# The x side of a gated recurrence: two four-step matmul groups become one eight-step block of seven half-width products

## The chip, the cores and the metric

One core of one Trainium2 chip runs the kernel. The metric is the device time of one execution in microseconds (us). The kernel before took 1693.7 us (median of three runs, 1693.68 to 1693.88). Differences within about 0.2% (3.4 us) are treated as no change.

## The reference

A gated recurrence runs over 512 steps for a batch of 8, with 512 inputs and a state h of 512 values, all float32. Its output is added to the input.

```
def step(h, x_t):
    fused = sigmoid(concat([x_t, h]) @ w_W + w_b)            # 1024 x 1024
    r, z = split(fused, 2)
    memory = x_t @ wx_W + wx_b + r * (h @ wh_W + wh_b)
    h_new = z * h + (1 - z) * tanh(memory)
return x + all h_new
```

Each step so needs an x side (x_t times the upper half of `w_W` and `wx_W`: 512 x 1536, which depends on nothing but the input) and an h side (h times the lower half of `w_W` and `wh_W`: 512 x 1536, which depends on the step before).

## The kernel before, in words

**Layout.** The 512 units are split into four quarters k of 128 (the contraction, on partitions) and each output of 512 into four parts j of 128. A matmul has 32 columns of data as its stationary operand and weights as its moving one, and writes partitions 32j to 32j+31 of PSUM. So four matmuls with j = 0 to 3 use four different column groups of TensorE, and every loop over j (`for j in range(NQ)`) issues four of them in a row. All matmuls go through the helper `mm`, line 178. Float32 matmuls leave two records each, a weight load and a matmul twice.

**h side, once a step.** `ORDER` is "R0 R1 G0 G1 R2 R3 G2 G3 H0 H1 H2 H3": three PSUM banks (R: the reset gate; G and H: the update gate and h @ wh) times four k, four matmuls of 128 columns each, 48 a step. Quarters 0 and 1 of the state lie in tile hTA, 2 and 3 in hTB.

**x side.** The x of four steps times 8 rows makes the 32 stationary columns of a *group* g. `prefill(g)` issues 16 matmuls of 384 columns (k = 0 to 3, j = 0 to 3) into columns 64 to 447 of the PSUM bank `xps[g % 2]`, which ScalarE has filled with the bias before (`seed`, line 213, a copy of 128x512). The x side is written out as a generator, `later`, and is worked off in program order behind the h side: after H3 of each step `take(later, 1)` issues the four matmuls of one k; step 0 takes four such. ScalarE later copies columns of `xps` into the R, G and H banks of the group (`spread`, line 230, 128x128 each, one a step for three steps), and VectorE transposes its X columns into `md1` (`turn_x`, line 235). The matmuls of the h side then add to what lies in R, G and H.

**The recurrence.** In each step, VectorE and ScalarE turn PSUM into the next state, in a fixed order: transposes of R (`tr`, line 303), sigmoid on ScalarE (line 205) into md0A and md0B, transposes of G (`md1A`, line 321, and `tz`), a scan that makes memory for half A (line 283), tanh, and a scan that makes the new hTA. Half B follows in the same way with H. R0 of the next step waits for hTA, R2 and R3 for the two parts of hTB. At the end of a step ScalarE does two copies of the new state and then the `spread` or `seed` of that step; VectorE does `turn_x` and three tiny memsets (line 383); GpSimd adds x to the new state for the output (line 385, two additions of 128x16). `turn_r` of half B waits for GpSimd's additions of eight steps before.

The order on every engine is written by hand (`manual_schedule`).

Of the kernel before, what the change touches and what calls it, by code (L numbers as in the profile page):

```python
# [7 lines left out]
F32 = mybir.dt.float32  # L8
BF16 = mybir.dt.bfloat16
AF = mybir.ActivationFunctionType  # L10
ALU = mybir.AluOpType
PSUM = bass.MemoryType.PSUM

P = 128
NQ = 4
GS = 4
B = 8
# [11 lines left out]
FIRST = "Q0 x Q1 x Q2 x Q3 H0 H1 H2 H3"  # L29

BANKS = ("R", "G", "H")

XP = {"G": slice(0, 128), "R": slice(128, 256), "X": slice(256, 384), "H": slice(384, 512)}

# [2 lines left out]
def tile_cond_rnn_residual(  # L37
# [39 lines left out]
    nc = tc.nc  # L77
    NCH = x.shape[0]
    T = NCH * TC
    NG = T // GS  # L80

    const = ctx.enter_context(tc.tile_pool(name="const", bufs=1))
# [13 lines left out]
    def load_x(c, half=slice(0, 2)):  # L96

        if c < NCH:
            if c not in xins:
                xins[c] = xin_p.tile([P, 2, NQ, TC * B // 2], F32, tag="xin", name=f"xin_{c}")  # L100
            nc.sync.dma_start(
                out=xins[c][:, half], in_=x[c].rearrange("p (e k n) -> p e k n", e=2, k=NQ)[:, half]
            )

    def x_of(c, k, t, n):

        e, t = divmod(t, TC // 2)
        if c == 0 and e == 0:
            first = head[:, :NX].rearrange("p (k n) -> p k n", k=NQ)
            return first[:, k, t * B : (t + n) * B]  # L110
        return xins[c][:, e, k, t * B : (t + n) * B]
# [6 lines left out]
    wx = const.tile([P, NQ, NQ, 384], F32, name="wx")  # L118
# [10 lines left out]
    def wh(bank, k, j):  # L129
        return whh[:, k, j] if bank == "H" else wgr[:, k, j, {"G": slice(0, 128), "R": slice(128, 256), "Q": slice(0, 256)}[bank]]  # L130
# [3 lines left out]
    def pair(n, name, rows, slots):  # L134

        if n == "A":
            return const.tile([P, rows, 2, slots], F32, name=name)
        return const.tile([P, 2, rows, slots], F32, name=name).rearrange("p c n s -> p n c s")
# [7 lines left out]
    md1 = [[pair(n, f"md1{n}{i}", 32, 2) for i in range(2)] for n in "AB"]  # L146
# [15 lines left out]
        nc.gpsimd.memset(t_[:, :, :, 1], -1.0)  # L162
    idle = const.tile([P, IDLE], F32, name="idle")

    def state(hf, i, slot=2):

        s = i % GS
        return hT[hf][i % NH][:, B * s : B * s + B, :, slot]

    ctx.enter_context(tc.manual_schedule())  # L170
    banks = [
        {n: psum.tile([P, 128], F32, name=f"{n}{q}") for n in BANKS}
        for q in range(2)
    ]
    xps = [psum.tile([P, 512], F32, name=f"xp{q}") for q in range(2)]

    def mm(out_, lhsT, rhs, start=False):
        nc.tensor.matmul(  # L178
            out_, lhsT, rhs, start=start, stop=False, skip_group_check=True
        )  # L180
# [4 lines left out]
    def warm():  # L185

        mm(xps[1], zeros[:, :128], zeros)
# [4 lines left out]
    bias = const.tile([P, 512], F32, name="bias")  # L192
    nc.vector.tensor_copy(bias, xps[0])
    for hf in range(2):
        for slot in (0, 2):
            nc.vector.tensor_copy(
                state(hf, 0, slot), hin[:, 2 * hf : 2 * hf + 2].rearrange("p c b -> p b c")
            )
# [12 lines left out]
    def seed(g):  # L211

        nc.scalar.copy(xps[g % 2], bias)

    def prefill(g):

        c, t0 = divmod(g * GS, TC)
        for k in range(NQ):
            for j in range(NQ):
                mm(  # L220
                    xps[g % 2][32 * j : 32 * j + 32, 64:448],
                    x_of(c, k, t0, GS),
                    wx[:, k, j, :],
                )
            yield

    def spread(g, names):

        for n in names:
            nc.scalar.copy(banks[g % 2][n], xps[g % 2][:, XP[n]])  # L230

    def turn_x(g, e):

        c0 = XP["X"].start + 32 * e
        nc.vector.transpose(
            md1[e // 2][g % 2][:, :, e % 2, 1], xps[g % 2][:, c0 : c0 + 32]
        )

    def take(it, n=None):
        while n is None or n > 0:  # L240
            if next(it, it) is it:
                return
            n = None if n is None else n - 1

    def x_side():
        for g in range(1, NG):
            yield from prefill(g)

    seed(1)
    take(prefill(0))  # L250
    warm()
    later = x_side()
    spread(0, "RGH")
    for e in range(NQ):
        turn_x(0, e)

    pool_done = {}
    for i in range(T):
        g, s = divmod(i, GS)
# [6 lines left out]

        for n in (ORDER if i else FIRST).split():
            if n == "x":
                take(later, 1)
                continue  # L270
            bank, k = n[0], int(n[1])
            hs = hT[k // 2][i % NH][:, :, k % 2, 2]
            for j in range(NQ):
                to = xps[0][:, :256] if bank == "Q" else ps[bank]
                mm(to[32 * j : 32 * j + 32, :], hs, wh(bank, k, j))
        take(later, 1)

        rows = slice(B * s, B * s + B)

# [57 lines left out]
        def memory(hf):  # L337

            m = work.tile([P, B, 2, 2] if hf == 0 else [P, 2, B, 2], F32, tag=f"m{hf}", name=f"m{hf}_{i}")
            if hf == 1:  # L340
                m = m.rearrange("p c n s -> p n c s")
            for c_ in scans(hf, m, md0[hf][g % 2][:, rows], md1[hf][g % 2][:, rows]):
                act(("n", hf, c_.start, i % NH), state(hf, i, 1)[:, :, c_], m[:, :, c_, 1], AF.Tanh)
# [16 lines left out]
        if i == T - 1:  # L360
            nc.gpsimd.tensor_tensor(
                ot[:, t, :2, :].rearrange("p c n -> p n c"),
                x_of(c, slice(0, 2), t, 1).rearrange("p c n -> p n c"),
                state(0, T),
                ALU.add,
            )
# [6 lines left out]
        if i < 3:  # L373
            load_x(i + 1)

        if g + 1 < NG:
            turn_x(g + 1, s)
            if s < 3:
                spread(g + 1, "RGH"[s])
            elif g + 3 < NG:  # L380
                seed(g + 3)
        for n in range(IDLE):
            nc.vector.memset(idle[:, n : n + 1], 0.0)
        def add(hf, engine):
# [97 lines left out]
```

## Time and profile before

| what | value |
|---|---|
| median of the runs | 1693.7 us |
| profiled execution: span from its first to its last instruction | 1691.7 us |
| outside the span, against the median of the runs | 2.0 us |
| TensorE matmul records busy | 1680.3 us, 99% of the span |
| VectorE busy | 1087.0 us, 64% |
| ScalarE busy | 915.5 us, 54% |
| GpSimd busy | 231.2 us, 14% |
| granted TensorE clock | 1.000 |

PE is TensorE's matmuls, PEld its weight loads, DVE is VectorE, ACT is ScalarE, POOL is GpSimd. A row of the timeline is the start in us, the length in us, then engine, source line, operation, output and inputs, shape and the number of records that were merged into it; in brackets stands how long the engine was idle before, and what ended that. The length of a row of matmuls holds the pipeline's depth too, so rows overlap; the distance between two starts is what counts.

### The profile page before, as it was taken

How to read it: one execution, taken by the hardware profiler on the slowest of the kernel's cores; microseconds unless marked ns; L12 is line 12 of the kernel's file. 1: busy time of each engine (PE TensorE's matmuls, PEld its weight loads, DVE VectorE, ACT ScalarE, POOL GpSimd, SP SyncE). 2: the span in 40 equal slices, each digit the busy share in tenths (PEclk: the TensorE clock that was granted, in tenths of full speed). 3: DMA queues.
4: the chain of work that ended last, by engine and by line, in shares of the span. 5: the costliest groups of instructions: out<-in, count | busy, mean ns of one | idle time of the engine just before them, and what ended most of it. 6: DMA issues, size and time to landing. Idle time of an engine off the chain costs nothing.

```text
span 1691.7 us, 121258 instructions
## 1 busy us (share of the span) xinstructions
PE 1680.3 (99%) x53230; PEld 1467.6 (87%) x53230; DVE 1087.0 (64%) x8229; ACT 915.5 (54%) x5121; POOL 231.2 (14%) x1032
## 2 busy tenths in 40 slices
PE   8999999999999999999999999999999999999998
PEld 6888888888888888888888888888888888888887
DVE  5666666666666666666666666666666666666666
ACT  3555555555555555555555555555555555555554
POOL 0111111111111111111111111111111111111111
PEclk9999999999999999999999999999999999999999
DMA  4000000000000000000000000000000000000000
GB/s 177 17 17 5 17 17 17 17 4 17 17 17 17 4 17 17 17 17 13 9 18 17 17 17 4 17 17 17 17 5 17 17 17 17 4 17 11 11 11 10
DMA packets 11483, 30.86 MB, mean 18 GB/s; under 512 B 1220, under 2 KB 1732, under 8 KB 10952
## 3 DMA queue, kind: packets, MB, share of 16 engines
q1 hardware_dynamic: 10800, 22.94, 3.9%
q8 instruction: 416, 6.82, 1.7%
q14 instruction: 115, 0.94, 0.2%
q10 hardware_dynamic: 152, 0.16, 0.0%
HBM read 14.70 MB, written 8.39 MB: 14 GB/s over the span
## 4 chain that ended last, share of the span: by engine, by line
PE 98%; DMA 1%; DVE 0%; ACT 0%; issue 0%; SPq 0%
PE R L178 26%; PE G L178 26%; PE H L178 26%; PE xp L178 19%; DMA whh<-in_whh_dram 1%; DMA head<-in_xh_dram 0%; DVE md1A L321 0%; DVE hTA L283 0%; ACT hd0A L205 0%; ACT hTA L205 0%; SPq L124 0%; DVE tz L303 0%; ACT hTB L205 0%; DVE hTB L283 0%; ACT hd0B L205 0%
## 5 line engine op out<-in xcount | busy, mean ns | idle before, releaser
L178 PE MATMUL xp<-wx,xin 128*32 128x384 f32 x4032 | 431.3, 486 | 0.0
L178 PEld LDWEIGHTS R<-wgr,hTA 128*32 128x32 f32 x8176 | 247.4, 135 | 206.8 <-DVE hTA L283 206.4
L303 DVE STREAM_TRANSPOSE tr<-R 128x64 f32<-128x64 f32 x1022 | 194.4, 229 | 309.1 <-PE R L178 309.1
L178 PE MATMUL R<-wgr,hTA 128*32 128x128 f32 x8176 | 330.9, 273 | 2.2 <-DVE hTA L283 2.2
L178 PE MATMUL H<-whh,hTA 128*32 128x128 f32 x8192 | 331.3, 273 | 0.8 <-DMA whh<-in_whh_dram 0.8
L178 PE MATMUL H<-whh,hTB 128*32 128x128 f32 x8192 | 331.2, 273 | 0.0
L178 PE MATMUL R<-wgr,hTB 128*32 128x128 f32 x8176 | 330.6, 273 | 0.0
L178 PE MATMUL G<-wgr,hTB 128*32 128x128 f32 x8176 | 330.6, 273 | 0.0
L178 PE MATMUL G<-wgr,hTA 128*32 128x128 f32 x8176 | 330.6, 273 | 0.0
L385 POOL TENSOR_TENSOR ot<-xin,hTB 128x16 f32<-128x16 f32 x503 | 126.4, 251 | 1415.6 <-DVE hTB L283 1324.0
L205 ACT ACTIVATE hd0B<-tz 128x16 f32<-128x16 f32 x512 | 114.9, 224 | 305.3 <-DVE tz L303 305.3
L205 ACT ACTIVATE md0A<-tr 128x16 f32<-128x16 f32 x512 | 119.6, 234 | 265.2 <-DVE tr L303 265.2
L178 PEld LDWEIGHTS H<-whh,hTA 128*32 128x32 f32 x8192 | 260.2, 136 | 1.2 <-DMA whh<-in_whh_dram 1.2
L178 PEld LDWEIGHTS G<-wgr,hTA 128*32 128x32 f32 x8176 | 259.8, 136 | 0.0
L178 PEld LDWEIGHTS H<-whh,hTB 128*32 128x32 f32 x8192 | 254.5, 122 | 0.0
L178 PEld LDWEIGHTS G<-wgr,hTB 128*32 128x32 f32 x8176 | 254.1, 122 | 0.0
L178 PEld LDWEIGHTS R<-wgr,hTB 128*32 128x32 f32 x8176 | 245.2, 122 | 0.0
L283 DVE TENSOR_TENSOR_SCAN hTA<-hd0A,hTA 128x48 f32<-128x48 f32 x512 | 132.1, 258 | 149.2 <-ACT hTA L205 149.2
L283 DVE TENSOR_TENSOR_SCAN hTB<-hd0B,hTB 128x24 f32<-128x24 f32 x1024 | 158.1, 196 | 104.0 <-ACT hTB L205 104.0
L205 ACT ACTIVATE hd0A<-tz 128x16 f32<-128x16 f32 x512 | 118.9, 232 | 111.4 <-DVE tz L303 111.4
L321 DVE STREAM_TRANSPOSE md1A<-G 128x64 f32<-128x64 f32 x511 | 156.8, 307 | 28.7
L205 ACT ACTIVATE hTB<-hTB 128x16 f32<-128x16 f32 x512 | 121.2, 237 | 81.1 <-DVE hTB L283 80.5
(62 smaller groups left out, 1680.2 us busy)
## 6 DMA issues: line engine op xcount, KB each, us to landing
xin<-in_x_dram SPq DMA_DIRECT2D x31, 256.0 KB, 3.8
out_dram<-ot SPq DMA_DIRECT2D x31, 256.0 KB, 3.3
wx<-in_wx_dram SPq DMA_DIRECT2D x4, 768.0 KB, 7.2
wgr<-in_wgr_dram SPq DMA_DIRECT2D x4, 512.0 KB, 9.7
whh<-in_whh_dram SPq DMA_DIRECT2D x1, 768.0 KB
whh<-in_wh_dram SPq DMA_DIRECT2D x1, 256.0 KB, 11.2
out_dram<-ot SPq DMA_DIRECT2D x1, 192.0 KB, 1.9
head<-in_xh_dram ACTq DMA_DIRECT2D x1, 144.0 KB, 5.2
```

Source lines behind the costliest of these rows:

```text
L178: nc.tensor.matmul(out_, lhsT, rhs, start=start, stop=False, skip_group_check=True)
L205: inst = nc.scalar.activation(out_, in_, func, **kw).ins
L283: nc.vector.tensor_tensor_scan(*[t_[:, :, c_].rearrange("p n c s -> p (n c s)") for t_ in (out_, d0, d1)], 0.0, ALU.mult, ALU.add,)
L303: inst = nc.vector.transpose(t_.rearrange("p c n -> p (c n)"), raw[n][hf]).ins
L321: nc.vector.transpose(md1[hf][g % 2][:, :, :, 0].rearrange("p n c -> p c n"), raw["h"][hf])
L385: return engine.tensor_tensor(ot[:, t, 2 * hf : 2 * hf + 2, :].rearrange("p c n -> p n c"), x_of(c, slice(2 * hf, 2 * hf + 2), t, 1).rearr ...
```

## The change

The change works on blocks of eight steps (two groups) instead of four. Write x of the block as four blocks x_nk (n: first or second four steps; k: first or second half of the 512 inputs) and the weights as four blocks w_kc (k as before; c: columns 64 to 255 or 256 to 447, 192 each). The four results x_n0 w_0c + x_n1 w_1c take eight products in the old way. The new way takes seven products of sums of blocks, and adds results to one another:

- GpSimd makes four sums of weights once, in steps 0 to 3 (`weight_sum`, 128x1536 each), and four sums of x for each block (`x_sum`, 128x64 each, in the last four steps of the block two before).
- `products(o)` issues seven products of 2 k times 4 j matmuls of 192 columns, 56 for a block. They go to four regions, AL and BE in `xps[0]`, GA and DE in `xps[1]`.
- What the products share is carried by ScalarE's copies from region to region (AL from the bias, DE from a difference of biases, BE from AL, GA from BE, each 128x192) and by GpSimd's additions of the SBUF tile `both` (a copy of DE) to `even` and `odd`, which hold the second 192 columns of a group in SBUF.
- `turn_x` and the `spread` of H read `even` and `odd` instead of PSUM.
- Groups 0 to 3 keep the old `prefill`. Steps 0 to 4 take two of its k each where before they took one (step 0 has three more before that, as before), and from step 5 on each step takes seven of the 56 matmuls, so that j goes on from where the last step left it: 0 1 2 3 0 1 2, then 3 0 1 2 3 0 1, and so on.

```
+def products(o):
+    t_ = [q[o % 2] for q in sx]
+    for to, lhs, rhs in (
+        (AL, x_half(o, 0, 0), wx_of(0, 0)),
+        (DE, t_[0], tw[0]),
+        (BE, t_[1], tw[1]),
+        (AL, x_half(o, 0, 1), wx_of(1, 0)),
+        (GA, t_[2], tw[2]),
+        (BE, t_[3], wx_of(1, 1)),
+        (GA, x_half(o, 1, 1), tw[3]),
+    ):
+        for k in range(2):
+            for j in range(NQ):
+                mm(reg(to)[32 * j : 32 * j + 32], lhs[:, k], rhs[:, k, j])
+                yield
...
 def x_side():
-    for g in range(1, NG):
-        yield from prefill(g)
+    for o in range(2, NG // 2):
+        yield from products(o)
...
-        take(later, 1)
+        if i < 5:
+            take(first[(i + 3) // 2], 2)
+        else:
+            take(later, 7)
...
+        o, u = divmod(i, 2 * GS)
+        nxt, two = o + 1 < NG // 2, o + 2 < NG // 2
+        if i == 0:
+            nc.scalar.copy(odd[0], xps[1][:, 256:512])
         if g + 1 < NG:
             turn_x(g + 1, s)
-            if s < 3:
-                spread(g + 1, "RGH"[s])
-            elif g + 3 < NG:
-                seed(g + 3)
+        if i == 0:
+            spread(1, "R")
+        if u == 0:
+            spread(2 * o + 1, "G")
+            if o and nxt:
+                nc.scalar.copy(reg(GA), reg(BE))
+        elif u == 1:
+            spread(2 * o + 1, "H")
+        elif u == 2 and o == 0:
+            seed(3)
+            nc.scalar.copy(even, xps[0][:, 256:512])
+        elif u == 2 and nxt:
+            last = odd[(o + 1) % 2][:, :HALF]
+            nc.scalar.copy(last, reg(GA))
+            nc.gpsimd.tensor_tensor(last, last, both, ALU.add)
+        elif u == 3 and nxt:
+            if o:
+                nc.scalar.copy(even[:, :HALF], reg(BE))
+                nc.gpsimd.tensor_tensor(even[:, :HALF], even[:, :HALF], both, ALU.add)
+            spread(2 * o + 2, "R")
+        elif u == 4 and nxt:
+            if o == 0:
+                nc.scalar.copy(odd[1], xps[1][:, 256:512])
+            spread(2 * o + 2, "G")
+            if two:
+                nc.scalar.copy(reg(AL), bias[:, AL[1]])
+                x_sum(o + 2, 0)
+        elif u == 5 and nxt:
+            spread(2 * o + 2, "H")
+            if two:
+                nc.scalar.copy(reg(DE), step_bias)
+                x_sum(o + 2, 1)
+        elif u == 6 and two:
+            nc.scalar.copy(reg(BE), reg(AL))
+            x_sum(o + 2, 2)
+        elif u == 7 and nxt:
+            spread(2 * o + 3, "R")
+            if two:
+                nc.scalar.copy(both, reg(DE))
+                x_sum(o + 2, 3)
+        if i < 4:
+            weight_sum(i)
+        if i == 4:
+            nc.gpsimd.tensor_tensor(step_bias, bias[:, BE[1]], bias[:, AL[1]], ALU.subtract)
```

`reg` picks a region of `xps`; `weight_sum(n)` and `x_sum(o, n)` are one GpSimd addition or subtraction each, of two blocks or of a block and a sum made before.

More of the change, by code (lines that the diff above doesn't have):

```diff
@@ L31 @@
 BANKS = ("R", "G", "H")
+HALF = 192
+AL, BE = (0, slice(64, 256)), (0, slice(256, 448))
+GA, DE = (1, slice(64, 256)), (1, slice(256, 448))
 XP = {"G": slice(0, 128), "R": slice(128, 256), "X": slice(256, 384), "H": slice(384, 512)}
@@ L163, in tile_cond_rnn_residual @@
     idle = const.tile([P, IDLE], F32, name="idle")
+    tw = [const.tile([P, 2, NQ, HALF], F32, name=f"tw{n}") for n in range(4)]
+    sx = [[const.tile([P, 2, GS * B], F32, name=f"sx{n}{q}") for q in range(2)] for n in range(4)]
+    step_bias = const.tile([P, HALF], F32, name="stepbias")
+    even = const.tile([P, 256], F32, name="even")
+    odd = [const.tile([P, 256], F32, name=f"odd{q}") for q in range(2)]
+    both = const.tile([P, HALF], F32, name="both")
     def state(hf, i, slot=2):
@@ L225, in prefill, with late, reg, wx_of @@
             yield
+    def late(g):
+        if g == 0:
+            return xps[0][:, 256:512]
+        return even if g % 2 == 0 else odd[g // 2 % 2]
     def spread(g, names):
         for n in names:
-            nc.scalar.copy(banks[g % 2][n], xps[g % 2][:, XP[n]])
+            src = late(g)[:, 128:256] if n == "H" else xps[g % 2][:, XP[n]]
+            nc.scalar.copy(banks[g % 2][n], src)
     def turn_x(g, e):
-        c0 = XP["X"].start + 32 * e
         nc.vector.transpose(
-            md1[e // 2][g % 2][:, :, e % 2, 1], xps[g % 2][:, c0 : c0 + 32]
+            md1[e // 2][g % 2][:, :, e % 2, 1], late(g)[:, 32 * e : 32 * e + 32]
         )
+    def reg(r):
+        return xps[r[0]][:, r[1]]
+    def wx_of(kh, ch):
+        return wx[:, 2 * kh : 2 * kh + 2, :, HALF * ch : HALF * ch + HALF]
+    def x_half(o, n, kh):
+        return x_of(o // 2, slice(2 * kh, 2 * kh + 2), 8 * (o % 2) + GS * n, GS)
+    def weight_sum(n):
+        a, b = [
+            (wx_of(0, 1), wx_of(0, 0)),
+            (wx_of(1, 1), tw[0]),
+            (wx_of(1, 1), wx_of(0, 1)),
+            (wx_of(1, 0), tw[1]),
+        ][n]
+        nc.gpsimd.tensor_tensor(tw[n], a, b, ALU.subtract)
+    def x_sum(o, n):
+        t_ = [q[o % 2] for q in sx]
+        a, b, op = [
+            (x_half(o, 1, 0), x_half(o, 1, 1), ALU.add),
+            (t_[0], x_half(o, 0, 0), ALU.subtract),
+            (x_half(o, 0, 0), x_half(o, 1, 0), ALU.subtract),
+            (x_half(o, 0, 1), t_[1], ALU.subtract),
+        ][n]
+        nc.gpsimd.tensor_tensor(t_[n], a, b, op)
+    def products(o):
+        t_ = [q[o % 2] for q in sx]
+        for to, lhs, rhs in (
[11 more added lines that the diff above has]
+                    yield
     def take(it, n=None):
@@ L252, in tile_cond_rnn_residual @@
     later = x_side()
+    first = {g: prefill(g) for g in (1, 2, 3)}
     spread(0, "RGH")
@@ L268, in tile_cond_rnn_residual @@
             if n == "x":
-                take(later, 1)
+                take(first[1], 1)
                 continue
@@ L275, in tile_cond_rnn_residual @@
                 mm(to[32 * j : 32 * j + 32, :], hs, wh(bank, k, j))
-        take(later, 1)
+        if i < 5:
+            take(first[(i + 3) // 2], 2)
+        else:
+            take(later, 7)
         rows = slice(B * s, B * s + B)
```

## The prediction, on record before the changed kernel was run

> **What bounds the kernel now.** I read the page's first part and the waits, then the timeline of one step in the middle, then the last steps, which have no x side.
>
> ```profile
> PE 1680.3 (99%) x53230; PEld 1467.6 (87%) x53230; DVE 1087.0 (64%) x8229; ACT 915.5 (54%) x5121; POOL 231.2 (14%) x1032
> ```
> ```profile
> PEld R L178 <- DVE hTA L283: 206.4, 510, 0.6
> ...
> PE R L178 <- DVE hTA L283: 2.2, 6, 0.4
> ```
>
> TensorE looks like the bound: its matmuls wait for the state 2.2 us in all. But the loads of R's weights (here the state is the stationary operand) wait for hTA in 510 steps, 0.4 us each: TensorE is only busy because x matmuls lie there. How long they cover it is seen in one step (matmuls, then loads):
>
> ```profile
> 799.52 0.86 PE L178 MATMUL xp<-wx,xin 128*32 128x384 f32 x8
> 800.16 0.65 PE L178 MATMUL R<-wgr,hTA 128*32 128x128 f32 x16
> 800.60 0.65 PE L178 MATMUL G<-wgr,hTA 128*32 128x128 f32 x16
> ...
> 802.78 0.86 PE L178 MATMUL xp<-wx,xin 128*32 128x384 f32 x8
> 803.43 0.43 PE L178 MATMUL R<-wgr,hTA 128*32 128x128 f32 x8
> ```
> ```profile
> 800.08 0.48 PEld L178 LDWEIGHTS R<-wgr,hTA 128*32 128x32 f32 x16 [0.40 <-DVE hTA L283]
> ...
> 803.35 0.38 PEld L178 LDWEIGHTS R<-wgr,hTA 128*32 128x32 f32 x12 [0.41 <-DVE hTA L283]
> ```
>
> A step takes 3.265 (record by record, in every one of some 490 steps), 2.62 of it for twelve rounds of h (800.16 to 802.78) and 0.645 for one round of x. The state comes in time for the load to start 0.08 before R's first matmul. So two things end almost together: TensorE's work, and the loop from R over VectorE and ScalarE back to hTA. The last steps show the loop alone, after the x side has run out:
>
> ```profile
> 1675.00 0.43 PEld L178 LDWEIGHTS R<-wgr,hTA 128*32 128x32 f32 x16 [0.62 <-DVE hTA L283]
> 1675.00 0.68 PE L178 MATMUL R<-wgr,hTA 128*32 128x128 f32 x16 [0.37 <-DVE hTA L283]
> ...
> 1678.23 0.43 PEld L178 LDWEIGHTS R<-wgr,hTA 128*32 128x32 f32 x16 [0.63 <-DVE hTA L283]
> 1678.24 0.67 PE L178 MATMUL R<-wgr,hTA 128*32 128x128 f32 x16 [0.37 <-DVE hTA L283]
> ...
> 1681.46 0.43 PEld L178 LDWEIGHTS R<-wgr,hTA 128*32 128x32 f32 x16 [0.62 <-DVE hTA L283]
> ```
>
> Without any x matmul a step still takes 3.23 (3.217 to 3.235 in five of them, mean 3.224). **The whole x side is worth 0.041 us a step, not 0.645.** All that a smaller x side can bring is 0.041 x 496 steps = 20 us.
>
> **What the change does to TensorE.** A record of 128 columns costs 0.109 (800.16 to 800.60 is four records deep in each of the four column groups), one of 384 columns 0.3225 (0.645 / 2). The straight line between them gives 0.1625 for 192 columns, so a new matmul (two records) is 0.325, an old one 0.645. A block of eight steps has 14 new matmuls per column group, 4.55 us, against 8 old ones, 5.16: 0.61 saved in each of 62 blocks, 38 us, if TensorE's sum were the time. It isn't, for two reasons.
>
> First, the loop's floor above. Second, seven matmuls do not fill four column groups evenly: in each step three groups get two (0.650) and one gets one (0.325). A group with two needs 2.62 + 0.65 = **3.270**, 0.005 longer than now. The group with one stands idle after 2.945 until the state comes. It can start R only then, so its surplus of 0.325 isn't carried over; it gains only the gap between its restart and the others'. The restart comes 3.21 to 3.224 after the start of the latest group in the step before. The upper end is the last steps' period. For the lower one, 803.35 is 3.14 after the latest group's start (800.16 and 0.047, record by record); to this come 0.05 from load to matmul (a first record after a wait is 0.05 longer than the others) and 0.02 for the order in which four groups are loaded.
>
> The short group moves on by one column each step (3, 2, 1, 0). In the slowest chain of steps a group restarts once and is then bound by its own work three times, and this repeats every four steps: (3.21 to 3.224 + 3 x 3.270) / 4 = 3.255 to 3.2585 a step. Against 3.265 this is 0.0065 to 0.010 less, times 496 steps: **3.2 to 5.0 us gained.** It needs the column groups to run apart, which no step of this trace tries, since all work comes in rows of four. For it speaks that after a wait the four groups start 0.007 apart, and in the middle of the run 0.031, 0.038 and 0.047 behind the first, each keeping its own beat for hundreds of steps; also that a matmul's second record starts after the first records of the other three. If groups can't pass one another, the price is in the second rival.
>
> The Trainium skill (TensorE: Matmul & The Clock Gate, Part 3, The mechanism) states that matmuls start and end strictly in program order, and that only weight loads are pulled ahead. By that rule the short group waits for its turn behind the others, nothing is gained, and the sum would be that rival's. The trace doesn't settle it: it keeps the rows in the order of their starts.
>
> **The first steps.** Groups 1 to 3 are computed early, in the old way: steps 0 to 4 take two k where they took one. Five rounds more of 0.645: **3.2 us lost.** That is work drawn forward, and it would come back if TensorE's sum were the bound; here three steps more without x at the end give back 3 x 0.041 = 0.1.
>
> **ScalarE.** The copies cost 0.265 for 128 columns and 0.591 for 512, so about 0.32 for 192:
>
> ```profile
> L213 ACT COPY xp<-bias 128x512 f32<-128x512 f32 x127 | 75.0, 591 | 4.8 <-DVE bias L193 4.6 <-ACT hTB L205 0.2
> L230 ACT COPY R<-xp 128x128 f32<-128x128 f32 x128 | 33.9, 265 | 3.1 <-PE xp L178 3.1
> ```
>
> Eight steps had six of 128 and two of 512; they get six of 128 and seven of 192, at most one pair a step, 0.59, no more than the one seed copy of today. That copy runs from 801.19 to 801.78, and the next sigmoid starts at 802.02, so it is covered; beyond 0.83 a step every ns would go into the loop. After seed steps the load's lead is 80.6 ns instead of 85: take 0.004 for each step, a quarter of which (one restart in four) is 0.5 us over the run. Step 4 has 0.95 of copies: 0.2 once, hidden in its longer x side.
>
> **GpSimd.** Per block four sums of 64 elements and two of 192; in steps 0 to 3 one of 1536 each. The nearest rows are its 128x16 addition (0.25) and two memsets:
>
> ```profile
> L160 POOL MEMSET hTB<- 128x192 f32 x1 | 0.3, 297 | 0.3 <-POOLq L466 0.3
> L162 POOL MEMSET hd0A<- 128x16 f32 x2 | 0.2, 120 | 1.8 <-DVE hd0A L160 1.2 <-DVE hd0B L160 0.5
> ```
>
> They give 1 ns an element. I take twice that for two inputs: 0.35, 0.6 and 3.3 us. From below 0.25 each; from above the addition's 0.25 / 16 an element, 1.0, 3.0 and 24 us, which the memset row makes unlikely. GpSimd has 3.27 - 0.46 free in each step and eight steps of slack towards `turn_r`; `even` is needed by `turn_x` some 2.6 us after its sum begins, and behind `turn_x` lie 0.6 us before R's transposes. Even 3.0 is hidden. The four weight sums end by about 35 us at 3.3 each; the first is needed in step 6, at some 43 us. At 24 each TensorE would stall some 45 us once.
>
> **The waits added.** Products wait for copies that end about 1 us before, and for sums made a step or more earlier. Behind the first product of a step are the rest of x and R; both waits end long before. `turn_x` waits for GpSimd and ScalarE, some 2 us early. Reads of SBUF in place of PSUM: 0 to 0.03 less on VectorE, off the loop. No DMA is moved; 1488 matmuls more fetch some more instructions, covered.
>
> **Sum.** 1691.7 (span) - 4.1 (the middle of 3.2 to 5.0) + 3.2 - 0.1 + 0.5 = 1691.2, and with the 2.0 around it 1693.2: no change.
>
> **Rivals.**
>
> - *A larger lead* (12%). The short group restarts earlier, or gains spread to the loop. With the floor of 3.224 in every step: 1693.7 - 20 + 3 = 1677. TensorE's full 38 us, 1656, would need the last steps' floor not to hold. Against it: three groups of four have more work per step than today. 1688 is as likely an end as 1677.
> - *Column groups can't pass* (20%), the other side. TensorE starts matmuls in program order, so R begins together in all groups. Every step then costs 3.270: 0.005 x 496 = 2.4, and the first steps 3.2: 1699.3. It decides as soon as the short group is held for the others' second product. For it: rows of four everywhere, so nothing shows the opposite; against it: the separate beats.
> - *The loop grows* (10%). GpSimd's 192-element sums in steps 2 and 3 of a block push its additions from 801.1 to 802.2 and later, over the scan for half A (802.52). One late addition did overlap two scans of half B, which took 170 and 168 ns against 172 on average, so I expect nothing. With 0.2 more in two steps of eight, less some 0.06 of lead: 124 x 0.14 = 17 us, 1711. It decides from 0.06 on.
> - *The seven products don't shorten TensorE's work*, since 192 columns cost a fixed sum more: each 10 ns per record make three groups 0.04 slower a step, 20 us, up to 1714. The line through 128, 256 (0.215) and 384 columns leaves no room; counted with the third.
>
> **Chances.** The forecast 58%. Changes under 0.2% (3.4 us) can't be told from none by measurement. Faster by more: 0.12. Slower: 0.30 (second and third rivals). The range leaves out the far ends of the first and third and takes in the second: 1689.5 to 1700.
>
> **What would show it.** Right: no matmul waits long, but the load of R still waits for hTA; a block of eight steps takes 26.04 to 26.07 us; the short group's R starts some 0.03 to 0.06 ahead of the others; steps 0 to 4 end 3.2 later than before. Wrong: steps of 3.20 (the loop is shorter than the last steps show), steps of 3.270 all alike (groups can't pass), or steps 2 and 3 of a block longer than the rest (GpSimd).

## The result, and the profile after

The changed kernel takes **1708.6 us** (median of four runs, 1708.2 to 1709.7) against 1693.8 in the same session: a ratio of 1.0089, with a 95% interval of [1.0076, 1.0101] (the ratio as recorded, which need not be the quotient of the two medians). It is 15 us slower. The forecast was 1693.2, no change, in a range that ended at 1700. The profiled execution took 1708.2, its span is 1705.7, 14.0 longer than before.

The engines' line and the waits of the page of before come back so, now with the changed kernel (engine, waiting tile and line, what ended the wait: us in total, times, longest):

```profile
PE 1688.3 (99%) x56206; PEld 1586.5 (93%) x56206; DVE 1104.8 (65%) x8229; ACT 963.4 (56%) x5434; POOL 381.1 (22%) x1409
```
```profile
PEld R L190 <- DVE hTA L353: 29.6, 76, 2.1
...
PE R L190 <- DVE hTA L353: 7.8, 13, 1.4
ACT hTA L217 <- DVE m L353: 6.8, 3, 2.3
```

The last line is new: three times ScalarE waits 2.3 us for a scan of VectorE. R's loads are listed with fewer waits for hTA than before (76, not 510) because more and shorter products lie ahead of them: the idle time before R's first load is now 0.11 us (median), too short to be listed, where it was 0.4. VectorE has the same 8229 instructions as before and is busy 17.8 us longer. The groups by form say which of them grew. Before and after, the scan that makes memory for half A, and then GpSimd's and ScalarE's new groups (busy us, mean ns, idle before):

```profile
L283 DVE TENSOR_TENSOR_SCAN m<-md0A,md1A 128x32 f32<-128x32 f32 x512 | 115.0, 225 | 0.0
```
```profile
L353 DVE TENSOR_TENSOR_SCAN m<-md0A,md1A 128x32 f32<-128x32 f32 x512 | 130.9, 256 | 0.0
...
L286 POOL TENSOR_TENSOR sx<-xin 128x64 f32<-128x64 f32 x124 | 39.9, 322 | 0.0
L466 POOL TENSOR_TENSOR odd<-odd,both 128x192 f32<-128x192 f32 x62 | 37.0, 598 | 204.4 <-ACT odd L465 204.4
...
L477 ACT COPY xp<-bias 128x192 f32<-128x192 f32 x62 | 20.0, 323 | 2.0
...
L275 POOL TENSOR_TENSOR tw<-wx,tw 128x1536 f32<-128x1536 f32 x2 | 7.0, 3476 | 0.0
```

This one scan took 15.9 us more in all, of the 17.8. Where it grew is seen in two stretches of the timeline. First the start, with the second of the four weight sums:

```profile
20.87 3.48 POOL L275 TENSOR_TENSOR tw<-wx,tw 128x1536 f32<-128x1536 f32 x1
21.99 2.43 DVE L353 TENSOR_TENSOR_SCAN m<-md0A,md1A 128x32 f32<-128x32 f32 x1
24.45 0.22 ACT L217 ACTIVATE hTA<-m 128x16 f32<-128x16 f32 x1 [2.17 <-DVE m L353]
```

The scan begins 1.1 us into GpSimd's sum and ends at 24.42, 0.08 after the sum (24.34, record by record). So it is in steps 1, 2 and 3 (2.43, 2.56, 2.56 us), each time under a long sum; the first of the four sums ends before these steps. The transposes of G that VectorE does under the same sums take 311 to 317 ns, against 311 on average. Then step 4 of a block, any block:

```profile
824.92 0.59 POOL L470 TENSOR_TENSOR even<-even,both 128x192 f32<-128x192 f32 x1 [2.25 <-ACT even L469]
...
825.47 0.25 POOL L499 TENSOR_TENSOR ot<-xin,hTB 128x16 f32<-128x16 f32 x1
...
825.67 0.24 POOL L499 TENSOR_TENSOR ot<-xin,hTA 128x16 f32<-128x16 f32 x1
...
825.87 0.32 POOL L286 TENSOR_TENSOR sx<-xin 128x64 f32<-128x64 f32 x1
825.92 0.35 DVE L353 TENSOR_TENSOR_SCAN m<-md0A,md1A 128x32 f32<-128x32 f32 x1
```

GpSimd's `even` sum, which waited for ScalarE's copy, pushes the two output additions and the first x sum of step 4 so far back that this x sum starts just ahead of the scan. The sum ends at 826.19, the scan at 826.27. In 59 of the 61 blocks where the two meet the scan ends so, 0.08 after the sum. In the other two the sum started 0.018 and 0.026 after the scan, and it is the sum that took longer, 0.35 in place of 0.32:

```profile
511.39 0.23 DVE L353 TENSOR_TENSOR_SCAN m<-md0A,md1A 128x32 f32<-128x32 f32 x1
511.41 0.35 POOL L286 TENSOR_TENSOR sx<-xin 128x64 f32<-128x64 f32 x1
```

From load to load of R (record by record) the steps of a block after step 0, 1, ... 7 are 3.271, 3.228, 3.278, 3.273, **3.414**, 3.226, 3.267 and 3.272: 26.228 a block, against 8 x 3.265 = 26.120 before. That is 0.108 x 61 blocks = 6.6 us. The first five such intervals are 5.696, 5.610, 5.553, 3.646 and 3.489, together 7.4 us more than before. The two make up the 14.0.

What was forecast of TensorE is there too. In the rows of matmuls, the short column group's R stands ahead of the rest:

```profile
819.63 0.65 PE L190 MATMUL xp<-tw,sx 128*32 128x192 f32 x9
819.98 0.33 PE L190 MATMUL xp<-wx,sx 128*32 128x192 f32 x2
...
820.14 0.33 PE L190 MATMUL xp<-wx,sx 128*32 128x192 f32 x2
820.22 0.69 PE L190 MATMUL R<-wgr,hTA 128*32 128x128 f32 x16
```

Record by record, R's first matmuls start at 820.216 and then at 820.277, 820.301 and 820.308. The last three stand one record of 192 columns (0.1625) behind the last x records of three groups (820.115, 820.139, 820.146), so the first is the short group's. And the last steps, without x side, have the period they had:

```profile
1688.66 0.42 PEld L190 LDWEIGHTS R<-wgr,hTA 128*32 128x32 f32 x16 [0.63 <-DVE hTA L353]
...
1691.88 0.43 PEld L190 LDWEIGHTS R<-wgr,hTA 128*32 128x32 f32 x16 [0.62 <-DVE hTA L353]
...
1695.10 0.43 PEld L190 LDWEIGHTS R<-wgr,hTA 128*32 128x32 f32 x16 [0.62 <-DVE hTA L353]
```

### The profile page after: what moved, and what is told of

Read it like the earlier page. It is cut to its first block, busy times and chain, and to the rows that moved or that the text cites. A ratio compares the mean times of both kernels' runs of the same rounds, so it can differ in the third digit from the quotient of the medians.

```text
span 1705.7 us, 128265 instructions
## 1 busy us (share of the span) xinstructions
PE 1688.3 (99%) x56206; PEld 1586.5 (93%) x56206; DVE 1104.8 (65%) x8229; ACT 963.4 (56%) x5434; POOL 381.1 (22%) x1409
## 4 chain that ended last, share of the span: by engine, by line
PE 97%; DVE 1%; DMA 1%; ACT 0%; issue 0%; SPq 0%
PE R L190 27%; PE G L190 26%; PE H L190 26%; PE xp L190 19%; DMA whh<-in_whh_dram 1%; DVE m L353 0%; DMA head<-in_xh_dram 0%; DVE md1A L391 0%; DVE hTA L353 0%; ACT hTA L217 0%; ACT hd0A L217 0%; DVE tz L373 0%; SPq L129 0%; ACT hTB L217 0%; DVE hTB L353 0%
## 5 line engine op out<-in xcount | busy, mean ns | idle before, releaser
L190 PE MATMUL R<-wgr,hTA 128*32 128x128 f32 x8176 | 351.8, 277 | 7.8 <-DVE hTA L353 7.8
L190 PE MATMUL H<-whh,hTA 128*32 128x128 f32 x8192 | 326.2, 273 | 0.7 <-DMA whh<-in_whh_dram 0.7
L190 PE MATMUL G<-wgr,hTA 128*32 128x128 f32 x8176 | 325.6, 273 | 0.0
L190 PE MATMUL G<-wgr,hTB 128*32 128x128 f32 x8176 | 325.5, 273 | 0.0
L190 PEld LDWEIGHTS R<-wgr,hTA 128*32 128x32 f32 x8176 | 232.7, 137 | 77.6 <-DVE hTA L353 29.6
L190 PEld LDWEIGHTS H<-whh,hTB 128*32 128x32 f32 x8192 | 248.9, 122 | 0.1
L190 PEld LDWEIGHTS G<-wgr,hTB 128*32 128x32 f32 x8176 | 248.4, 122 | 0.0
L190 PEld LDWEIGHTS R<-wgr,hTB 128*32 128x32 f32 x8176 | 229.3, 122 | 0.3
L190 PE MATMUL xp<-tw,sx 128*32 128x192 f32 x2976 | 217.2, 326 | 0.0
L190 PE MATMUL xp<-wx,xin 128*32 128x192 f32 (+1 forms) x2048 | 168.8, 331 | 0.0
```

The source lines that it names most:

```text
L190: nc.tensor.matmul(out_, lhsT, rhs, start=start, stop=False, skip_group_check=True)
```

## The experiments

The theory: GpSimd's sums hold up VectorE's scan for half A, by three of the four long ones at the start and one short one in step 4 of each block, and the rest of the change does what was forecast. The rivals: the loop is longer for another reason in those steps (TensorE's uneven products, ScalarE's copies, a wait on GpSimd), and the long scan is only where the delay shows. A time stands with its ratio to the kernel before in the same session and the 95% interval.

**e1, the x sum one step later.**

```
             if two:
                 nc.scalar.copy(reg(AL), bias[:, AL[1]])
-                x_sum(o + 2, 0)
         elif u == 5 and nxt:
             spread(2 * o + 2, "H")
             if two:
                 nc.scalar.copy(reg(DE), step_bias)
+                x_sum(o + 2, 0)
                 x_sum(o + 2, 1)
```

> The first x sum of a block is made one step later (with the second one, in step 5 of a block instead of step 4). Theory 1 (a VectorE scan that starts while a GpSimd addition runs ends only after it): the scan for half A in step 4 of a block goes back from 372 ns to 225 ns, the 3.41 us step goes back to about 3.27, a block from 26.23 us to 26.04 to 26.10, so 8 to 11 us less in 62 blocks: 1698 to 1701 us. Theory 2 (seven matmuls over four column groups, or ScalarE's copies, make the steps longer): 1708 to 1709 us, as the change.

Measured: 1699.25, 1.0034 [1.0021, 1.0047], 9.3 less than the change. The scan in step 4 is back at 225 ns, that step at 3.269, and the block takes 26.073. In 123 steps here the scan starts while an output addition still runs for up to 0.07 us, and it takes its 225 ns all the same: an addition that ends early in the scan costs nothing.

**e2, no weight sums**, and **e3, both.** e2 leaves the four weight sums out and lets the products read blocks of the weights in their place, so that the x side from step 16 on is not the reference's. e3 adds e1's edit.

```
-            (DE, t_[0], tw[0]),
+            (DE, t_[0], wx_of(0, 1)),
...
-        if i < 4:
-            weight_sum(i)
```

> The four weight sums are left out; four products read blocks of wx in their place, so the x side is not the reference's from step 16 on, with matmuls of the same number and size. Theory 1: the scans for half A in steps 1 to 3 go back from 2.4 to 2.6 us to 0.23, these steps go from 5.70, 5.61 and 5.55 us to 3.91 (the two rounds of x that lie in them), 5 us less: about 1703.5 us. Theory 2: no difference, 1708 to 1709 us.

> Both edits together: x sum one step later, weight sums left out (the x side is not the reference's from step 16 on). Theory 1: both gains add up and what is left is the forecast without GpSimd, 1693 to 1696 us, a block 26.04 to 26.10 us against 26.12 of the kernel before. Theory 2: over 1700 us.

Measured: e2 1703.09, 1.0057 [1.004, 1.0073], 5.5 less than the change; e3 1693.74, 1.0004 [0.9995, 1.0013], 14.85 less, which is 9.3 + 5.5. With both sums out of the scan's way the kernel stands where the forecast had it. The same scan in e1, e2 and e3, by group:

```profile
L353 DVE TENSOR_TENSOR_SCAN m<-md0A,md1A 128x32 f32<-128x32 f32 x512 | 121.9, 238 | 0.0
```
```profile
L353 DVE TENSOR_TENSOR_SCAN m<-md0A,md1A 128x32 f32<-128x32 f32 x512 | 124.4, 243 | 0.0
```
```profile
L353 DVE TENSOR_TENSOR_SCAN m<-md0A,md1A 128x32 f32<-128x32 f32 x512 | 115.1, 225 | 0.0
```

**e4, the delay made in the kernel before.** Nothing of the change but two useless GpSimd additions behind the output additions of every eighth step; the second lies over the scan.

```
+        if i % 8 == 3:
+            nc.gpsimd.tensor_tensor(spare[:, :192], bias[:, :192], zeros[:, :192], ALU.add)
+            nc.gpsimd.tensor_tensor(spare[:, :320], bias[:, :320], zeros[:, :320], ALU.add)
```

> The kernel before with two GpSimd additions more in every eighth step, behind the output additions: 128x192 and 128x320 into a tile that nobody reads, some 0.6 and 0.9 us, from about 1.5 us after R's load to 2.9; the scan for half A starts at 2.45. Nothing waits for them. Theory 1: the scan ends with the addition, about 0.3 us late, less 0.03 of lead, 64 times: 1708 to 1713 us. Theory 2 (GpSimd beside VectorE costs nothing): 1693.7 us.

Measured: 1714.05, 1.0119 [1.0104, 1.0135].

```profile
824.17 0.60 POOL L408 TENSOR_TENSOR spare<-bias,zeros 128x192 f32<-128x192 f32 x1
824.86 0.87 POOL L409 TENSOR_TENSOR spare<-bias,zeros 128x320 f32<-128x320 f32 x1
825.23 0.58 DVE L284 TENSOR_TENSOR_SCAN m<-md0A,md1A 128x32 f32<-128x32 f32 x1
```

The addition ends at 825.73, the scan at 825.81; the step takes 3.620. Nobody waits for `spare`: the overlap alone costs it. The time is just over the 1708 to 1713 that were expected. None of the rivals' causes is in this kernel, so they fall here.

**e5, one addition that ends before the scan.** As e4 with the second addition alone.

> The kernel before with one GpSimd addition of 128x320 more in every eighth step, behind the output additions: about 0.9 us, from 1.45 us after R's load to 2.35, so it ends before the scan for half A starts at 2.45. Theory 1 (only an addition over the scan costs): 1693.5 to 1694.5 us, scan 225 ns. Theory 2 (any GpSimd work beside VectorE costs, or the work itself): 1700 us or more.

Measured: 1693.82, 1.0 [0.999, 1.001], with the same scan 0.17 after the addition's end:

```profile
815.11 0.88 POOL L408 TENSOR_TENSOR spare<-bias,zeros 128x320 f32<-128x320 f32 x1
816.16 0.23 DVE L284 TENSOR_TENSOR_SCAN m<-md0A,md1A 128x32 f32<-128x32 f32 x1
```

**e8 and e9, what kind of instruction holds the scan.** In the kernel before, e8 puts a memset of 1280 elements there; e9 puts by turns a copy of 1536 elements (one input) and a memset of 2048.

```
+        if i % 16 == 3:
+            nc.gpsimd.tensor_copy(spare[:, :1536], wx[:, 0, :, :])
+        if i % 16 == 11:
+            nc.gpsimd.memset(spare, 0.0)
```

> The kernel before with a GpSimd memset of 128x1280 (some 1.4 us, from 1.45 us after R's load to 2.9) in every eighth step, over the scan for half A. It writes and reads nothing. If any GpSimd instruction holds the scan up: scan about 0.5 us in that step, some 1706 us. If only instructions that read SBUF do: scan 225 ns, 1693.7 us.

> The kernel before, with one GpSimd instruction behind its output additions in every eighth step, over the scan for half A: by turns a copy of 1536 elements with one input, and a memset of 2048 elements. Neither result is used. If any long GpSimd instruction holds the scan until it ends, the scan of half A takes over 0.6 us in both kinds of step, where it takes 0.225 in the others, and the time is some 1705 to 1715 us. If only an instruction that reads SBUF does, the scan is long in the steps with the copy and 0.225 in those with the memset, and the time is about 1700. If it takes two inputs on GpSimd, the scan is 0.225 everywhere and the time 1693.8.

Measured: e8 1693.83 (one run; its memset of 1.17 us met only the first 0.1 us of the scan, so it tells little), e9 1700.55 (one run).

```profile
817.87 1.47 POOL L408 COPY spare<-wx 128x1536 f32<-128x1536 f32 x1
818.93 0.48 DVE L284 TENSOR_TENSOR_SCAN m<-md0A,md1A 128x32 f32<-128x32 f32 x1
```
```profile
844.20 1.81 POOL L410 MEMSET spare<- 128x2048 f32 x1
845.28 0.23 DVE L284 TENSOR_TENSOR_SCAN m<-md0A,md1A 128x32 f32<-128x32 f32 x1
```

All 32 scans under a copy took 467 to 484 ns; the 32 inside a memset took 224 to 227. So a GpSimd copy or addition, which reads SBUF, holds the scan, and a memset, which only writes, doesn't.

**e7, the change with its sums out of the way.** Three weight sums before step 0, the fourth in eight pieces of 192 elements behind the output additions of steps 0 to 7, and e1's edit.

```
+    for n in (0, 2, 1):
+        weight_sum(n)
...
+        if i < 8:
+            weight_sum(3, i)
```

**e6, e10 and e11, even columns.** On top of e7, the products are cut by columns so that all four column groups get the same work in a step: 336 columns in each (e6), or 384, 320, 320, 320 (e10) and 384, 384, 288, 288 (e11) over four steps. The finer the cut, the more matmuls: 58, 57 and 56 a step, where the change has 55 and the kernel before 52.

```
-                for j in range(NQ):
-                    mm(reg(to)[32 * j : 32 * j + 32], lhs[:, k], rhs[:, k, j])
-                    yield
+                c0 = 0
+                while c0 < HALF:
+                    c1 = min(HALF, c0 + left)
+                    for j in range(NQ):
+                        mm(reg(to)[32 * j : 32 * j + 32, c0:c1], lhs[:, k], rhs[:, k, j, c0:c1])
...
```

> As e6 but with the seven matmuls of the change: only GpSimd's sums are moved, nothing is left out. Theory 1: 1693 to 1696 us, blocks of 26.06 to 26.10 us, no scan over 0.3 us after step 0. Theory 2 (the weight sums cost wherever they lie): 1698 us or more.

> The change with three edits, a candidate that computes the reference: the x sum one step later, three weight sums before step 0 and the fourth in eight pieces of 128x192 behind the output additions of steps 0 to 7, and the 14 products of k cut by columns so that each step takes 336 columns in all four column groups (192 + 144, 48 + 192 + 96 and so on) instead of seven matmuls of 192. Theory 1 (uneven column groups keep three of four at 3.27 us, and the loop's floor is 3.22): x takes 0.57 to 0.62 us in every group, a step 3.22 to 3.24, a block 25.8 to 25.9 us, 1676 to 1682 us. Theory 2 (the loop, not the uneven groups, is what keeps the blocks at 26.07): 1692 to 1696 us.

> As e6_even_columns, with the columns of the x side cut 384, 320, 320, 320 over four steps in all column groups, nine pieces in four steps instead of ten: 57 matmuls a step instead of 58. If the gaps of e6 come from TensorE's instructions arriving too slowly, they depend on the number of matmuls in a step: at 57 there are clearly fewer of them, and the time lies between e7's 1696.5 and e6's 1745.8, some 1710 to 1730. If the gaps have another cause, one that only the uneven cut has, they stay at some 40 us, 1740 or more. Without any gap one step would take 3.27 and three 3.224, 1685.

> As e6_even_columns, with the columns cut 384, 384, 288, 288: eight pieces in four steps, 56 matmuls a step. Two steps of 3.27 and two of 3.224 are 3.247 a step, 0.018 less than before; with the 3 us that the early rounds cost, 1687 to 1691 us if no gaps come. If instructions arrive too slowly, some gaps remain, more than in e7 (55 matmuls a step, 2 us of gaps), and the time is 1693 to 1705.

Measured: e7 1696.50, 1.0017 [1.0007, 1.0026]; e6 **1745.79**, 1.0306 [1.029, 1.0321]; e10 1694.24, 0.9998 [0.9987, 1.0009]; e11 **1690.16**, 0.9979 [0.9969, 0.9988]. e11 is the one version that beats both kernels, the kernel before by 3.6 us, hardly more than the 3.4 that count as no change. e7 lies between its two expectations, and e10 under both of its own. e6 was a plain miss: its first steps run at 3.21 to 3.23, and from some 60 us on TensorE has gaps, 96 of over 0.25 us, that nothing visible ends. Waits of the weight loads in e6, then in e11 ("issue" is time in which the engine waited for nothing that the profile shows):

```profile
PEld xp L192 <- issue: 19.3, 57, 1.7
PEld H L192 <- issue: 15.5, 45, 0.7
PEld R L192 <- DVE hTA L370: 14.1, 57, 0.6
PEld G L192 <- issue: 9.9, 35, 0.7
PEld R L192 <- issue: 7.7, 31, 0.5
```
```profile
PEld R L192 <- DVE hTA L371: 37.4, 132, 0.6
PEld xp L192 <- issue: 4.8, 20, 0.6
```

All 96 of e6's gaps end 1.2 to 1.7 us after a packet of 16 KB of the instruction queue lands, and these packets come 3.7 us apart there, 4.0 in the kernel before. There is one packet for every 256 of TensorE's records (118529 records and 463 packets in e6). So I suspected that TensorE's instructions arrive too slowly.

**e12, e13 and e14, the same columns in more matmuls.** In the kernel before, each x matmul of 384 columns is cut: into three of 128, those of one column group in a row (e12); into three, in rows over the groups (e13); into two of 192, in rows (e14). 60, 60 and 56 matmuls a step, the same columns. Of e13:

```
-            for j in range(NQ):
-                mm(
-                    xps[g % 2][32 * j : 32 * j + 32, 64:448],
...
+            for n in range(0, 384, 128):
+                for j in range(NQ):
+                    mm(
+                        xps[g % 2][32 * j : 32 * j + 32, 64 + n : 192 + n],
...
```

> The kernel before with each x matmul of 384 columns cut into three of 128: 60 matmuls a step instead of 52, the same columns, nothing else. Three records of 0.109 against one of 0.3225 are 0.654 a round instead of 0.645: 0.009 more in 496 steps, 1698 us by the sum of TensorE's work. If TensorE's instructions arrive no faster than one packet in some 3.5 us, 60 matmuls (240 instructions with their loads) in 3.27 us are more than arrive, gaps like those of e6 come, and the time is over 1730.

> The kernel before with each x matmul of 384 columns cut into three of 128, but issued in rows: one piece of each of the four column groups, then the next pieces. 60 matmuls a step as in e12. If e12's 194 us come from its order (three pieces of one column group in a row, so that the next group's lie behind them), they are gone here; by the sum of TensorE's work 0.009 a step is added, 1698 us. If TensorE gets its instructions too slowly for 58 matmuls in 3.22 us (e6), it does for 60 in 3.27 too, and gaps like those of e6 come: 1720 to 1760 us, with waits of the weight loads that nothing visible ends.

> The same with two pieces of 192 columns in rows: 56 matmuls a step, as many as in e11, which had one gap. Two records of 0.1625 for one of 0.3225 make 3.270 a step: 0.005 more in 496 steps, 1696 us, without gaps by both theories. Some 10 us more than that would mean that the cut itself costs something that the sum of records lacks.

Measured: e12 1888.21, 1.1146 [1.1129, 1.1163]; e13 1760.29, 1.0394 [1.0378, 1.0409]; e14 1698.20, 1.0026 [1.0016, 1.0036], 2 us over the 1696 that were expected; in its profiled run R's first load comes 1.3 us later than in the kernel before. e12 has no gaps; its steps are evenly 3.647 long, for another reason than the one it was made for. The loads of one step of e12:

```profile
800.81 0.17 PEld L178 LDWEIGHTS xp<-wx,xin 128*32 128x32 f32 x2
...
801.09 0.85 PEld L178 LDWEIGHTS xp<-wx,xin 128*32 128x32 f32 x19
801.84 0.21 PEld L178 LDWEIGHTS R<-wgr,hTA 128*32 128x32 f32 x5
```

The x side is spread over 1 us. Record by record, the first x matmuls of the four groups start at 800.871, 801.095, 801.343 and 801.592: a group's begin only when three of the six records of the group ahead have started. The four groups' R so starts at 801.840, 801.847, 802.023 and 802.271: the last one comes 0.43 behind the first, where it is 0.047 in the kernel before. The difference, 0.38, is what the step is longer (3.647 against 3.265). The state is not what the first group waits for: the scan that makes hTA ends at 801.69, and elsewhere R's load follows it by 0.05.

e13 shows e6's gaps, 92 of over 0.25 us, all ending 1.2 to 1.6 us after a packet, in the kernel before, with nothing changed but the number and width of the x matmuls; e14, with the same order and 56, has none. The loads' waits in e13:

```profile
PEld H L178 <- issue: 20.2, 51, 1.0
PEld R L178 <- issue: 8.8, 30, 1.0
PEld G L178 <- issue: 7.1, 25, 0.5
PEld xp L178 <- issue: 7.0, 22, 0.5
```

"Issue" waits of the weight loads in all, against the matmuls that a us would hold if there were no gaps (matmuls a step by the step's length by the sum), each of one profiled execution:

| kernel | matmuls a step | step by the sum, us | matmuls per us | "issue" waits, us |
|---|---|---|---|---|
| before | 52 | 3.265 | 15.9 | 3.0 |
| e7 | 55 | 3.2585 | 16.9 | 8.3 |
| e14 | 56 | 3.270 | 17.1 | 1.5 |
| e11 | 56 | 3.247 | 17.2 | 6.2 |
| e10 | 57 | 3.2355 | 17.6 | 9.4 |
| e6 | 58 | 3.224 | 18.0 | 52.4 |
| e13 | 60 | 3.274 | 18.3 | 43.1 |

Between 17.6 and 18.0 the gaps jump. e10 may vary there: its ten runs took 1688.2 to 1696.35, and the profiled one 1690.62. That more matmuls in a step bring the gaps, and that they end behind instruction packets, is shown. That it is a plain limit of the rate at which instructions arrive is not: from 200 to 1600 us, e6 with its gaps ran fewer matmul records a us (34.3) than e10 did almost without (35.0), and e10's packets came closer together (3.6 us) than e6's (3.7). What part of the supply runs dry stays open.

## Why the prediction was wrong, point by point

**The loop's floor: right.** The last steps take 3.22 to 3.23 as before, and no step of any of these kernels was much shorter.

**TensorE's products: right, with a gain just short of the forecast.** The block was to take 26.04 to 26.07; it took 26.073 in e1, with steps of 3.269, 3.228, 3.270, 3.270. The short group's R starts 0.061 ahead, against 0.03 to 0.06. The gain is (26.120 - 26.073) x 62 = 2.9 us, against 3.2 to 5.0.

The prediction weighed the Trainium skill's rule (TensorE: Matmul & The Clock Gate, Part 3, The mechanism) that matmuls start and end strictly in program order. These traces disagree on the starts of matmuls in different column groups: the short group's R starts ahead of the others' by 0.061 in the step shown and by 0.057 to 0.077 (medians) after every step of a block but step 4, where the scan is held up and all four groups wait, though which group is short changes from step to step; and in e12 up to three records of one group start after a record that lies behind them in the program.

**The first steps: the rounds right, the sums wrong.** In e3, without weight sums, three of the first intervals are 3.910, 0.645 over before, and the first five are 2.4 longer in all (2.6 in e2), against 3.2. The weight sums, put down as hidden, cost 4.9 in these intervals and 5.5 in the run (the change against e2).

**ScalarE: right in size.** The copies took 0.30 to 0.32 (0.32 was forecast), and e3, which has them all, is no slower than before. Their 0.5 us in the sum was not measured apart.

**GpSimd: the failed step.** The sums were sized well: 0.32, 0.60 and 3.47 us against 0.35, 0.6 and 3.3. But the step asked only who waits for their results ("Even 3.0 is hidden"), and no wait for one is listed. What it left out, and so put at nothing, is that a sum holds a VectorE scan on another tile until the sum ends: 9.3 us by the x sum of step 4 (e1), 5.5 by the weight sums (e2), 14.85 together (e3). With the two added, the forecast gives 1693.2 + 14.85 = 1708.05; 1708.6 was measured.

**The third rival had the mechanism** (GpSimd over the scan, 10%) at the wrong steps and size: it looked to the 192-element sums in steps 2 and 3 of a block, 17 us. Those end before the scan; it is the 64-element sum that they push back, 0.15 a block more. Its price came close (1711) by luck in part, since 5.5 of the 15 come from sums that it didn't name. What spoke against it was a poor row: the two scans of half B under a late addition (170 and 168 ns) met only its last 0.13 and 0.04 us. A scan of half B takes 0.053 less than one of half A, so by the 0.08 found here (an estimate) a hold would have ended it some 0.03 after the addition, at most 0.16 after its start: too little to show.

The Trainium skill has the rule that was missed (SBUF — State Buffer, SBUF: two separate sides): VectorE and GpSimd share a pair of ports, which whoever starts first holds for its whole instruction, and a VectorE instruction with two SBUF inputs contends for it only against a GpSimd instruction that reads SBUF. The runs agree in what they show: the scan (two inputs in SBUF) ends 0.08 after additions of 0.32, 0.87 and 3.47 us and a copy of 1.47, a memset doesn't touch it, and in the two blocks where the scan came first the sum was the one to take longer (0.35). The ports themselves are seen in no run here.

**The second rival** (groups can't pass, 1699.3) is ruled out by the 0.061.

**Steps of the prediction that no run settled:** "1488 matmuls more fetch some more instructions, covered" holds at 55 matmuls a step (e3 stands at 1693.74), but not three matmuls further, as e6 shows. Part of the spread of e7 (1695.0 to 1698.4 in ten runs) comes from there: its profiled run (1697.8) has five gaps of over 0.25 us, 2.1 us in all, each ending 1.4 to 1.6 us after a packet. The kernel before lies within 0.8 us in that session. e3 spreads too (1693.2 to 1697.6), but of the 3.1 us that its profiled run (1696.8) lies above its median 2.4 fall before step 1, whose R load comes at 21.87 us, against 19.44 in e2. Why it starts late stays open.

## What to carry to other kernels

When work goes to an idle engine, ask not only who waits for its result but what it shares with the engine on the critical path: lay each new GpSimd instruction against the VectorE instructions of that time in the timeline, and see which of them read two SBUF tensors. If it must be long, put it where no such instruction is due, or cut it into pieces that fit between them; moving one 0.32 us sum by a step gave back 9.3 us here. And where a kernel already issues matmuls densely, count them: fewer columns in more matmuls can cost more than the columns save.

## What the runs showed of the hardware that was not expected

- A VectorE scan with two SBUF inputs ends 0.08 us after a GpSimd addition or copy that began before it, however long that is (225 ns grew to 0.35, 0.48, 0.58 and 2.56 us). Additions that end in its first 0.07 us, and memsets, leave it at 225 ns.
- Column groups of TensorE run apart, but not far: a group whose turn lies behind matmuls of another group started when no more than three records of that group were still to start (e12).
- At 58 matmuls (116 records) in 3.22 us, TensorE had 40 us of gaps of over 0.25 us, all ending 1.2 to 1.7 us after an instruction packet; at 57 in 3.24 us it had 2.6.
